# One more odd product on VectorE in the scan steps that begin from zero

## The chip, the cores and the metric

The kernel runs on one core of one Trainium2 chip. The metric is the device time of one execution in microseconds (us); lower is better. Engines are named as in the profile: PE is TensorE's matmul and PEld its weight load, DVE is VectorE, ACT is ScalarE, POOL is GpSimd, SP is SyncE, which issues the DMAs.

## The reference, cut to what matters

Two layers work on 16 images of 64 x 64 points and 96 channels, in fp32. The first is a resampled MLP; the second is a two-dimensional selective scan. The change touches the second only. With the normalized image turned into 192 channels of a sequence of L = 4096 points, four directions k (rows and columns, each forward and backward) are scanned with 16 states per channel:

```
delta = softplus(dts + dt_bias)
h0 = zeros
def step(h, inps):
    dt, ut, bt, ct = inps
    h = exp(dt[..., None] * As[None]) * h + (dt * ut)[..., None] * bt[:, :, None, :]
    y = einsum('bkdn,bkn->bkd', h, ct)
    return h, y
```

The four results are added, normalized over the channels, gated and projected back.

## The kernel before, in words

**Steps.** The scan goes image by image. An image has 8 steps, `once`: four pieces of T = 1024 points with the two forward directions (`pair` 0), then the four pieces in reverse order with the two backward directions (`pair` 1). So 16 images make 128 steps. The first step of each direction pair, `st % NT == 0` with NT = 4, begins its scans from 0.0 (line 904); the other three begin from the column that the step before left in the small tile `new` (`states`). In this document the first step of an image (forward, line 906) is its *opening step* and the fifth (backward, line 908) its *turning step*.

**Units.** A step has 6 blocks (`bi`) of 4 units (`j` = 0 to 3, four states of the 16 each). They are counted 0 to 23 here, so that unit 5 is `bi` 1, `j` 1. One unit covers two groups of 32 channels, e = 0 and e = 1, and 128 partitions hold 32 channels times 4 states. Its work is:

- `drive` (line 897, POOL): b = dtu x B, 128 x 2048, made two units ahead, in one of four buffers.
- `decay` (line 891, ACT): da = exp(delta x A), 128 x 1024 for each e, into PSUM. There is one PSUM buffer for each e, so the next unit's decay waits until this unit's da has been read for the last time.
- `recur` (lines 906 and 908, DVE): the scan h = da x h + b, 128 x 1024, once for each e. For e = 0 the states are written over da in PSUM. For e = 1 they go over b in SBUF, except in units with `odd_here`, where they go over da too.
- The product with C: for e = 0 on DVE (line 1062). For e = 1, the "odd" product, on POOL (line 1045, into one of two `odd` buffers); only where `odd_here` holds, which is `j == 3`, on DVE (line 1052).
- `keep` (line 914): the last column of h is copied to the small tile. For e = 0 ACT does it; for e = 1 DVE, but ACT where `odd_here` holds.
- `read_out` (line 931, PE): sums over the states into a PSUM tile per block.

**Order.** The order on each engine is the order in which the loop of lines 1007 to 1086 is written. Three slots in each unit hold other work: `all_work` (the step sizes of coming blocks, lines 745 to 763: m, e, w, d on ACT, half of the sum in PE, dtu on DVE) and one background generator, `front` of the next image (group norm, MLP, convolution) or `finish` of the image before. They advance by units, not by time. In opening steps `front` comes to the group norm's end in units 10 and 11: ACT makes the scale (lines 270 to 296), PE `k_ps` (line 298), and DVE adds `shift` (line 312) between the two scans of unit 11. In turning steps ACT fills the padded image (line 501) around units 4 to 7.

**What a unit's queues look like.** Where `odd_here` does not hold, ACT's decay of the next unit's e = 1 is issued right behind this unit's first scan, and POOL has odd and then the drive of two units ahead. Where it holds, POOL has only the drive; ACT's copy and the decay of e = 1 come behind DVE's line 1052, at the place of DVE's copy.

Of the kernel before, what the change touches and what calls it, by code (L numbers as in the profile page):

```python
# [63 lines left out]
NT = L // T  # L64
NQ = 4
# [12 lines left out]
def tile_two_blocks(  # L78
# [125 lines left out]
    def send(kept=0):  # L204
        while len(put_off) > kept:
            args, kwargs = put_off.pop(0)
            nc.sync.dma_start(*args, **kwargs)
# [475 lines left out]
    def scan():  # L683


        with ExitStack() as es:
# [126 lines left out]
            def fetch_dtu(ctx, bi):  # L813
                t = p2.tile([128, 2, T], F32, name="dtu")
                for e in range(2):
                    spread(t[:, e, :], "dtu", ctx, bi, e)
                return t

            def fetch_delta(ctx, bi, e):
                t = p3.tile([128, T], F32, name="delta")  # L820
                spread(t, "delta", ctx, bi, e)
                return t
# [11 lines left out]
            def fetch_y0(lc, bi):  # L834
                y0 = yp.tile([128, 2 * QT], F32, name="y0")
                nc.sync.dma_start(out=y0, in_=ypart[lc, bi])
                return y0
# [50 lines left out]
            def decay(n, e):  # L888
                k, g = group(n, e)
                da = aps.tile([128, T], F32, name="da", tag=f"da{e}")  # L890
                nc.scalar.activation(da, deltas[n // NQ, e], AF.Exp, scale=a_s[:, k, g, units[n][2]:units[n][2] + 1])  # L891
                das[n, e] = da

            def drive(n):
                b = p4.tile([128, 2, T], F32, name="b")
                bt = bc[0, blocks[units[n][1]][2], units[n][2]]
                nc.gpsimd.tensor_mul(b, dtus[n // NQ], bt.unsqueeze(1).to_broadcast([128, 2, T]))  # L897
                bs[n] = b

            def recur(n, e, out):  # L900
                st, bi, j = units[n]
                pair = steps[st][1]
                da, b = das.pop((n, e)), bs[n][:, e, :]
                before = 0.0 if st % NT == 0 else states[bi][0][:, e, j:j + 1]
                if pair == 0:
                    nc.vector.tensor_tensor_scan(out, da, b, before, ALU.mult, ALU.add)  # L906
                else:
                    nc.vector.tensor_tensor_scan(out[:, ::-1], da[:, ::-1], b[:, ::-1], before, ALU.mult, ALU.add)  # L908

            def keep(n, e, h, copy):  # L910
                st, bi, j = units[n]
                if st % NT < NT - 1:
                    end = h[:, T - 1:T] if steps[st][1] == 0 else h[:, 0:1]
                    copy(states[bi][1][:, e, j:j + 1], end)  # L914
# [21 lines left out]
            def store(n):  # L936

                st, bi, _ = units[n]
                mi, pair, lc = steps[st]
                v, s0, r = blocks[bi]  # L940
                yt = yp.tile([128, 2, QT], F32, name="yt")
                nc.scalar.copy(yt, ys.pop(n // NQ))
                yield
                if pair == 0:
                    part = dram.tile([128, 2 * QT], F32, name="part", tag=f"part{lc}_{bi}")
                    ypart[lc, bi] = part
                    nc.sync.dma_start(out=part, in_=yt.rearrange("p e t -> p (e t)"))
                else:
                    g = s0 if v < 2 else 4
                    for q in range(NQ):  # L950
                        first = T * lc + QT * q
                        nc.sync.dma_start(
                            out=image[mi]["y"][r, 32 * g:32 * g + 64, first:first + QT].rearrange(
                                "(e c) t -> c e t", e=2
                            ),
                            in_=yt[32 * q:32 * q + 32, :, :],
                        )
# [33 lines left out]
            def slot(position):  # L991
                back = ahead_gen if ahead_gen.gen is not None else behind_gen
                next(work, None)
                back.at(position)
                if back is ahead_gen and back.gen is None and position == 2:
                    behind_gen.at(position)
# [10 lines left out]
            for n, (st, bi, j) in enumerate(units):  # L1007
                mi, pair, lc = steps[st]
                v, s0, r = blocks[bi]
                m = n // NQ  # L1010
                if n % per_image == 0:
                    image[mi]["y"] = dram.tile([2, DI, L], F32, name="y_d")
                    behind_gen.drain()
                    send()
                    ahead_gen = behind_gen = Background(None)
                    if mi + 1 < B:
                        ahead_gen = Background(front(mi + 1))
                elif n % per_image == 2 and mi > 0:
                    behind_gen = Background(finish(mi - 1))
                if j == 0:  # L1020
                    new = stp.tile([128, 2, NQ], F32, name="new", tag=f"st{bi}")
                    states[bi] = (states[bi][1] if states[bi] else None, new)

                if j == 0:
                    ahead = None
                    if bi + 1 < len(blocks):
                        ahead = ctxs[st], bi + 1
                    elif n + NQ <= last:
                        ahead = ctxs[st + 1], 0
                    if ahead:  # L1030
                        dtus[m + 1] = fetch_dtu(*ahead)


                odd_here = j == NQ - 1
                h = das[n, 1] if odd_here else bs[n][:, 1, :]
                recur(n, 1, h)
                if not odd_here:
                    decay(n + 1, 1)
                slot(0)
                if storing is not None:  # L1040
                    next(storing, 0)
                    storing = None
                if not odd_here:
                    odds[n] = po.tile([128, T], F32, name="odd")
                    nc.gpsimd.tensor_mul(odds[n], h, bc[1, r, j])  # L1045
                if n + 2 <= last:
                    drive(n + 2)

                states_of_odd, h = h, das[n, 0]
                recur(n, 0, h)  # L1050
                if odd_here:
                    nc.vector.tensor_mul(bs[n][:, 1, :], states_of_odd, bc[1, r, j])  # L1052
                    keep(n, 1, states_of_odd, nc.scalar.copy)
                    if n < last:
                        decay(n + 1, 1)
                else:
                    keep(n, 1, states_of_odd, nc.vector.tensor_copy)
                if n >= 1 and j == 0:
                    storing = store(n - 1)
                    next(storing)  # L1060
                slot(1)
                nc.vector.tensor_mul(bs[n][:, 0, :], h, bc[1, r, j])  # L1062
                keep(n, 0, h, nc.scalar.copy)
                if n < last:
                    decay(n + 1, 0)
                read_out(n)
                due = list(put_off)
                slot(2)
                for one in due:
                    if put_off and put_off[0] is one:  # L1070
                        send(len(put_off) - 1)
                if j < 2 and ahead:
                    deltas[m + 1, 1 - j] = fetch_delta(*ahead, 1 - j)
                if j == 1 and n + 3 <= last and steps[units[n + 3][0]][1] == 1:
                    st2, bi2, _ = units[n + 3]
                    y0s[steps[st2][2], bi2] = fetch_y0(steps[st2][2], bi2)


                at = n % per_step
                for what in range(2):  # L1080
                    ahead_j = at - (2 * NQ - 1 + what)
                    if 0 <= ahead_j < NQ:
                        bc[what, 1, ahead_j] = fetch_bc(ctxs[st], 1, ahead_j, what)
                    ahead_j = at - (5 * NQ - 1 + what)
                    if 0 <= ahead_j < NQ and st + 1 < len(steps):
                        bc[what, 0, ahead_j] = fetch_bc(ctxs[st + 1], 0, ahead_j, what)
# [114 lines left out]
```

## Time and profile before

| | |
|---|---|
| median of three runs | 20166.42 us (20149.25 to 20170.37) |
| the profiled execution | 20161.48 us, span 20159.7 us |
| line 897 POOL b, 128 x 2048, 3072 | 4544 ns each |
| line 1045 POOL odd, 128 x 1024, 2304 | 2366 ns each |
| lines 906, 908 DVE scans from `new`, 128 x 1024 | 2336 to 2341 ns each |
| lines 906, 908 DVE scans from 0.0, 1536 | 2277 to 2278 ns each |
| line 1062 DVE product, 3072 | 1220 ns each |
| line 1052 DVE product, 768 | 1205 ns each |
| line 914 copy: DVE 1728, ACT 2880 | 148 ns, 157 ns each |
| line 891 ACT decay, 6144 | 1116 ns each |

Rows of a timeline have the start (us from the span's start), the duration (us), engine, line, operation, output<-inputs, shapes, and in brackets the engine's idle time before the instruction with what ended it. The duration of one instruction reaches some 0.1 us into the next one of the same engine, so costs are taken from start to start. A bracket names the latest releaser that the profile can see, which is sometimes one that was long done.

### The profile page before, as it was taken

The page shows a single profiled execution, that of the slowest core. Times are in us where ns is not written, and L with a number is a line of the kernel's source. Part 1 is how long each engine was busy: PE and PEld are TensorE (multiplying, and loading weights), DVE is VectorE, ACT ScalarE, POOL GpSimd, SP SyncE. Part 2 cuts the span into 40 slices and gives each one's busy share as a digit, 9 for nine tenths or more (in the row PEclk, how much of TensorE's full clock was granted, in tenths as well). Part 3 has the DMA queues.
Part 4 walks back from the last instruction along what each step waited for, and adds up shares of the span by engine and source line. Part 5 has one row for each costly group of instructions (what it writes and reads, how often), then busy time and mean ns, then how long its engine had stood idle before and what let it go on. Part 6 is the DMA issues. An engine that isn't in the chain of part 4 may idle for free. (4 is left out here: it accounts for less than half of the span.)

```text
span 20159.7 us, 275360 instructions
## 1 busy us (share of the span) xinstructions
PE 16614.9 (82%) x98732; PEld 7202.4 (36%) x98732; DVE 19096.7 (95%) x12996; ACT 13337.4 (66%) x19798; POOL 19140.5 (95%) x5384
## 2 busy tenths in 40 slices
PE   7877888888888888888888888888888888888866
PEld 4423334343343433324333343433434333243222
DVE  1999999999999999999999999999999999999997
ACT  4666766667666666766667666676666667666554
POOL 0999999999999999999999999999999999999996
PEclk8887898988889898898988889888898888989977
DMA  2665666766667666676766667666676766767654
GB/s 88 215 231 205 231 233 219 241 220 229 232 220 247 211 238 224 226 240 215 245 216 231 235 218 243 218 230 236 219 246 208 238 224 225 243 214 243 231 204 156
DMA packets 1977337, 4478.63 MB, mean 222 GB/s; under 512 B 464798, under 2 KB 564030, under 8 KB 1973918
## 3 DMA queue, kind: packets, MB, share of 16 engines
q1 hardware_dynamic: 1975966, 4461.01, 64.9%
q8 instruction: 780, 12.78, 0.3%
q14 instruction: 591, 4.84, 0.1%
HBM read 3581.91 MB, written 878.18 MB: 221 GB/s over the span
## 5 line engine op out<-in xcount | busy, mean ns | idle before, releaser
L897 POOL TENSOR_TENSOR b<-dtu,bt 128x2048 f32<-128x2048 f32 x3072 | 13918.9, 4544 | 535.4 <-DMA dtu<-dtu_d 470.3
L891 ACT ACTIVATE da<-delta,a_s 128x1024 f32<-128x1024 f32 x6144 | 6853.0, 1116 | 2289.0 <-DVE b L1062 796.6
L1045 POOL TENSOR_TENSOR odd<-b,ct 128x1024 f32<-128x1024 f32 x2304 | 5451.7, 2366 | 323.5 <-DVE b L908 184.5
L931 PE MATMUL y<-b,fold_s 128*32 128x256 f32 x30720 | 2641.4, 439 | 2513.0 <-DVE b L1062 2493.7
L1062 DVE TENSOR_TENSOR b<-da,ct 128x1024 f32<-128x1024 f32 x3072 | 3747.6, 1220 | 13.7
L908 DVE TENSOR_TENSOR_SCAN da<-da,new,b 128x1024 f32<-128x1024 f32 x1440 | 3337.7, 2336 | 101.8 <-ACT da L891 86.1
L906 DVE TENSOR_TENSOR_SCAN da<-da,new,b 128x1024 f32<-128x1024 f32 x1440 | 3339.7, 2338 | 35.5 <-ACT da L891 15.2
L914 ACT COPY new<-da 128x1 f32<-128x1 f32 x2880 | 453.0, 157 | 3361.1 <-DVE b L1062 1827.9
L931 PEld LDWEIGHTS y<-b,fold_s 128*32 128x32 f32 x30720 | 745.0, 116 | 4733.7 <-DVE b L1062 2667.6
L908 DVE TENSOR_TENSOR_SCAN b<-da,new,b 128x1024 f32<-128x1024 f32 x864 | 2021.0, 2339 | 48.1 <-ACT da L891 47.9
L906 DVE TENSOR_TENSOR_SCAN b<-da,new,b 128x1024 f32<-128x1024 f32 x864 | 2022.6, 2341 | 0.0
L931 PE MATMUL y<-odd,fold_s 128*32 128x256 f32 x18432 | 1608.1, 422 | 125.6 <-POOL odd L1045 122.1
L534 PE MATMUL c_ps<-xgp,wtap_s 96*64 96x512 f32 (+1 forms) x4608 | 1651.8, 612 | 5.5 <-ACT xgp L501 5.5
L400 PE MATMUL h_ps<-wide,w1t_s 96*128 96x500 f32 x1920 | 1119.6, 695 | 179.8 <-ACT wide L407 100.7
L427 PE MATMUL o_ps<-w2c_s,wide 128*100 128x96 f32 x9600 | 1081.1, 279 | 96.6 <-ACT wide L407 95.3
L427 PEld LDWEIGHTS o_ps<-w2c_s,wide 128*100 128x100 f32 x9600 | 1038.7, 192 | 280.4 <-ACT wide L407 157.0
L908 DVE TENSOR_TENSOR_SCAN da<-da,b 128x1024 f32<-128x1024 f32 x480 | 1084.6, 2278 | 32.6 <-ACT da L891 21.8
L906 DVE TENSOR_TENSOR_SCAN da<-da,b 128x1024 f32<-128x1024 f32 x480 | 1085.4, 2277 | 22.4 <-ACT da L891 12.1
L755 PE MATMUL s<-w,ident_s 128*128 128x512 f32 x1534 | 946.5, 703 | 193.3 <-ACT w L753 191.5
L755 PE MATMUL s<-m,half_s 128*128 128x512 f32 x1534 | 1064.7, 783 | 1.0 <-ACT m L745 1.0
L738 PE MATMUL s<-pr,dtw_s 128*128 128x512 f32 x1536 | 1052.5, 773 | 0.0
L534 PEld LDWEIGHTS c_ps<-xgp,wtap_s 96*64 96x64 f32 (+1 forms) x4608 | 593.9, 168 | 945.4 <-issue 908.8
(141 smaller groups left out, 21917.2 us busy)
## 6 DMA issues: line engine op xcount, KB each, us to landing
dtu<-dtu_d SPq DMA_DIRECT2D x1536, 512.0 KB
delta<-delta_d SPq DMA_DIRECT2D x1536, 512.0 KB
bt<-rows SPq DMA_DIRECT2D x1024, 512.0 KB
ct<-rows SPq DMA_DIRECT2D x1024, 512.0 KB
u<-xs_d SPq DMA_DIRECT2D x1536, 256.0 KB
dtu_d<-dtu SPq DMA_DIRECT2D x767, 256.0 KB
delta_d<-delta SPq DMA_DIRECT2D x767, 256.0 KB
wide<-in_x SPq DMA_DIRECT2D x768, 128.0 KB
```

Of the source, the lines that this page charges most:

```text
L400: nc.tensor.matmul(h_ps[j], lhsT=w1t_s[:, 128 * j:128 * (j + 1)], rhs=xu.rearrange("c p q -> c (p q)"), start=True, stop=True,)
L427: nc.tensor.matmul(o_ps[:, p, :], lhsT=hsq[j][:, UPS * p:UPS * (p + 1)], rhs=w2c_s[:, j, :], start=(j == 0), stop=(j == HB - 1),)
L534: nc.tensor.matmul(c_ps[p:p + n], lhsT=wtap_s[:, tap, 128 * i:128 * i + n], rhs=xgp[:, h0:h0 + 8, dx:dx + HW], start=(tap == 0), stop=(tap ...
L738: nc.tensor.matmul(s, lhsT=dtw_s[:, pair, v, :], rhs=ctx["pr"][t], start=True, stop=False, skip_group_check=True)
L755: nc.tensor.matmul(s, lhsT=by, rhs=of, start=False, stop=(of is d), skip_group_check=True)
L891: nc.scalar.activation(da, deltas[n // NQ, e], AF.Exp, scale=a_s[:, k, g, units[n][2]:units[n][2] + 1])
L897: nc.gpsimd.tensor_mul(b, dtus[n // NQ], bt.unsqueeze(1).to_broadcast([128, 2, T]))
L906: nc.vector.tensor_tensor_scan(out, da, b, before, ALU.mult, ALU.add)
L908: nc.vector.tensor_tensor_scan(out[:, ::-1], da[:, ::-1], b[:, ::-1], before, ALU.mult, ALU.add)
L931: nc.tensor.matmul(y[32 * q:32 * q + 32, e, :], lhsT=fold_s, rhs=weighed[e][:, QT * q:QT * q + QT], start=(pair == 0 and j == 0 and e == 0 ...
L1045: nc.gpsimd.tensor_mul(odds[n], h, bc[1, r, j])
L1062: nc.vector.tensor_mul(bs[n][:, 0, :], h, bc[1, r, j])
```

## The change

`odd_here` holds in one more unit of the steps that begin from zero: unit 5 (`bi` 1, `j` 1). There the states of e = 1 are written over da in PSUM, their product with C is DVE's line 1052 instead of POOL's line 1045, the copy of their last column is ACT's instead of DVE's, and the decay of unit 6's e = 1 is issued behind that product. There are 32 such units.

```
-                odd_here = j == NQ - 1
+                odd_here = j == NQ - 1 or (st % NT == 0 and bi == 1 and j == 1)
                 h = das[n, 1] if odd_here else bs[n][:, 1, :]
                 recur(n, 1, h)
                 if not odd_here:
```

## The prediction

> **What bounds the kernel now.** I read the page's first part, then the busy time by windows for one step of each kind, then the timelines of VectorE (DVE), GpSimd (POOL) and ScalarE (ACT) around unit 5, the unit that changes. Unit numbers count the 24 of a step from 0; "opening" is a step that starts the forward scan of an image, "turning" one that starts the backward scan; only these two of eight begin from zero.
>
> The page: two engines share the first place.
>
> ```profile
> PE 16614.9 (82%) x98732; PEld 7202.4 (36%) x98732; DVE 19096.7 (95%) x12996; ACT 13337.4 (66%) x19798; POOL 19140.5 (95%) x5384
> ```
>
> The windows (stretch and its length, then busy time of each engine) of the opening step of the third image, the step behind it, and that image's turning step:
>
> ```profile
> 2892.50:3042.20 149.70, 109.54 (x806) 51.21 (x806) 145.53 (x106) 105.39 (x183) 146.38 (x43) 0.79 0.65 218
> 3042.20:3192.70 150.50, 129.75 (x946) 71.18 (x942) 148.54 (x104) 105.53 (x166) 150.50 (x43) 0.84 0.63 214
> 3490.40:3643.20 152.80, 120.37 (x668) 42.74 (x668) 145.85 (x108) 115.21 (x180) 149.61 (x43) 0.89 0.68 234
> ```
>
> The reader is to see that POOL never rests in the ordinary step (150.50 of 150.50), but idles 3.3 and 3.2 us in the two that the change touches: there POOL waits too. So what counts is where POOL next waits for DVE behind unit 5.
>
> **What is removed, added and moved.** 32 steps (two in each of 16 images) have one such unit. POOL loses one odd product: the row of line 1045 has 2366 ns, and from its start to the next start is 2.32 us (2926.54 to 2928.86). DVE loses a copy of one column and gains line 1052's product; ACT gains the copy (157 ns). The scan of e=1 now writes onto da in PSUM, so the next unit's decay of e=1 is issued behind the new product instead of behind that scan. No DMA is moved. TensorE's read-out of unit 5 follows DVE's last product instead of POOL's odd: from 2928.9 to about 2929.1, in the turning step from 3531.6 to 3532.9; nothing near waits for it.
>
> DVE in units 3, 4 (start) and 5 of that opening step; unit 3 has the form that unit 5 gets:
>
> ```profile
> 2913.78 1.20 DVE L1052 TENSOR_TENSOR b<-da,ct 128x1024 f32<-128x1024 f32 x1
> 2914.90 0.68 DVE L759 TENSOR_TENSOR dtu<-s,u 128x512 f32<-128x512 f32 x1
> 2915.50 1.21 DVE L1062 TENSOR_TENSOR b<-da,ct 128x1024 f32<-128x1024 f32 x1
> 2916.63 2.28 DVE L906 TENSOR_TENSOR_SCAN b<-da,b 128x1024 f32<-128x1024 f32 x1
> ...
> 2924.47 2.27 DVE L906 TENSOR_TENSOR_SCAN da<-da,b 128x1024 f32<-128x1024 f32 x1
> 2926.65 0.15 DVE L914 COPY new<-b 128x1 f32<-128x1 f32 x1
> 2926.78 1.22 DVE L1062 TENSOR_TENSOR b<-da,ct 128x1024 f32<-128x1024 f32 x1
> 2927.92 2.28 DVE L906 TENSOR_TENSOR_SCAN b<-da,b 128x1024 f32<-128x1024 f32 x1
> ```
>
> ACT beside it: copy and decay behind unit 3's product, then unit 5's stretch:
>
> ```profile
> 2915.02 0.16 ACT L914 COPY new<-da 128x1 f32<-128x1 f32 x1 [3.55 <-DVE b L1052]
> 2915.21 1.12 ACT L891 ACTIVATE da<-delta,a_s 128x1024 f32<-128x1024 f32 x1
> ...
> 2926.01 1.10 ACT L891 ACTIVATE da<-delta,a_s 128x1024 f32<-128x1024 f32 x1
> 2927.05 0.70 ACT L749 ACTIVATE w<-e,one_s 128x512 f32<-128x512 f32 x1
> 2927.66 0.71 ACT L750 ACTIVATE d<-e,one_s 128x512 f32<-128x512 f32 x1
> 2928.27 0.14 ACT L914 COPY new<-da 128x1 f32<-128x1 f32 x1
> 2928.44 1.12 ACT L891 ACTIVATE da<-delta,a_s 128x1024 f32<-128x1024 f32 x1
> ```
>
> DVE's delay by start-to-start times:
> - The product takes 1.12 (2913.78 to 2914.90), the copy gives back 0.13 (2926.65 to 2926.78): +0.99.
> - A new wait. The product starts at 2926.65; by unit 3's rows the decay starts 1.43 later (2915.21 - 2913.78), 2928.08, and ends 1.12 on, 2929.20. A scan that waits for a decay starts 0.10 after its end (turning step, 3526.04 to 3526.14). So unit 6's first scan starts at 2929.30, not 2927.92: +1.38. In unit 3 this wait is covered by line 759's product (0.60) between; unit 5 has none, so the wait shows with 0.39.
> - Queued behind that decay on ACT are w, d, the copy and the decay of e=0: its end is 3.55 behind the first decay's start (2926.01 to 2929.56), so 2931.63. The second scan could start at 2929.30 + 2.20 = 2931.50, and starts at 2931.66: +0.16. Sum **1.54 us**.
>
> The trace shows no product 1052 without 759 behind it, so the wait is bounded: below by 0 (d = 1.0), above by the 1.5 us that ACT's longest neighbouring pair takes (line 501, d = 3.0) if ACT were not free. I take 1.54, since ACT is idle when the product ends (its queue ends at 2926.01, in the turning step at 3530.25 against 3531.65).
>
> **What of it reaches the end, opening step.** POOL gets 2.32 ahead, but its next odd products need scans that are later. At unit 8 odd starts 1.57 after its scan's end (2943.07 to 2944.64); where it waits that is 0.13. 1.54 - 1.57 + 0.13 = +0.10: POOL's gain is gone at unit 8. From unit 6 to 10 DVE waits for nothing, and at unit 11 comes the wait that ends last:
>
> ```profile
> 2963.38 0.15 DVE L312 TENSOR_TENSOR shift<-k_ps,cb_s 96x1 f32<-96x1 f32 x1 [2.78 <-PE k_ps L298]
> ```
>
> and behind it POOL:
>
> ```profile
> 2971.08 2.35 POOL L1045 TENSOR_TENSOR odd<-b,ct 128x1024 f32<-128x1024 f32 x1 [1.56 <-PE y L931]
> ```
>
> (this odd starts 0.13 after its scan; the name in the bracket is of something long done). k_ps hangs on ACT's group norm and TensorE's queue; ACT last idled for DVE at 2946.55 (0.68 <- DVE b L1062, unit 8), so that chain inherits 1.54, and DVE's 0.50 wait for b at unit 11 does not shorten it. All engines are then 1.54 late. The first two images' opening steps have a 0.60 wait for b at unit 7 (1706.40) that takes up part: 0.94. The last image's has no such chain, but its odd of unit 16 waits for DVE (0.14): 1.54.
>
> **Turning step.** Odd products of POOL, unit 4 waiting and unit 8 almost:
>
> ```profile
> 3522.44 2.34 POOL L1045 TENSOR_TENSOR odd<-b,ct 128x1024 f32<-128x1024 f32 x1 [2.01 <-DVE b L908]
> ...
> 3547.36 2.36 POOL L1045 TENSOR_TENSOR odd<-b,ct 128x1024 f32<-128x1024 f32 x1
> ```
>
> Unit 8's scan ends at 3546.95 (3544.67 + 2.28), 0.41 ahead; 1.54 - 0.41 + 0.14 = 1.27, a little less by the other images' rows: 1.26. From there POOL works without rest to the step's end. One (from 10832.8) has unit 20 at 0.22 behind a decay wait: 1.45. The last image's has 1.6 at unit 8 and two 0.6 waits for b: POOL keeps 0.5 of its gain.
>
> The ordinary steps go on at POOL's rate, and nothing there waits for a clock time, so delays add: 13 x 1.54 + 2 x 0.94 + 1.54 + 14 x 1.26 + 1.45 - 0.5 = **42 us**. The profiled execution took 20161.5 (span 20159.7): 20203.5. It lies 4.9 below the median 20166.4, so 20208 by the median, +0.21%.
>
> The Trainium skill, "Perfetto Trace Analysis", section Identifying the Most-Contended Engine, would improve the engine of highest occupancy first; that is POOL here, and by it alone the change wins 2.32 x 32. The windows above speak against it: in these steps POOL idles.
>
> **Rivals.**
> - **POOL's 2.32 reaches the end**: -74, 20092. It needs 1.54 + 2.32 - 0.13 = 3.7 us between scan and odd at units 8 and 12. For: POOL is busy 149.6 of 152.8. Against: unit 8 has 1.57 and 0.41, unit 12 0.13.
> - **Stalls swallow DVE's delay** (not slower): if k_ps is set by ACT's and TensorE's own queues, the opening steps cost 0 to 0.5 and the turning ones 0.7 to 1.26 (d = 1.0 to 1.54): +10 to +28, mid 20185. For: ACT stands 0.43 late at unit 9's copy. Against: the 0.68 of idle ACT time at unit 8. It decides below 1.26 us a step.
> - **ACT comes later than DVE** (clearly slower): the decay of unit 6 starts 2.07 later (2926.01 to 2928.08), 0.53 more than d. If ACT's later waits at units 13 and 14 (0.9 and 1.1 us of DVE idle for da) return that in full, 32 x 0.53 = 17 to 23 more: 20225 to 20231. Against: ACT idles 1.21 at 2933.68.
>
> **How the numbers follow.** Forecast (+30 to +50) 0.60; swallowed 0.20; POOL's gain 0.08; ACT later 0.12. About 0.2%, 40 us, is what a measurement of this kernel can tell from no change. The forecast lies on that line, so I split it 0.34 slower, 0.26 within: slower 0.46, same 0.46, faster 0.08. The range leaves out POOL's gain and the ends of the others: from +6 (stalls swallow most) to +69 (ACT later, and a few us of scatter: the three runs spread 21): 20172 to 20235.
>
> **What would show it.** Right: 2272 products on line 1045 and 800 on 1052; behind unit 5's product an idle of 0.4 us of DVE <- ACT da; POOL's idle before unit 12 of opening steps grown from 1.5 to 3; opening and turning steps longer by 1.5 and 1.3, the six others alike. Wrong: turning steps shorter (POOL bound to the end), or opening steps unchanged with a shorter wait for k_ps.

## The result and the profile after

| | before | after |
|---|---|---|
| median of 15 runs each, same chip | 20166.58 us (20149.12 to 20177.75) | 20203.45 us (20187.80 to 20218.34) |
| the profiled execution, span | 20161.48, 20159.7 us | 20207.56, 20205.8 us |

The ratio is 1.0020, with a 95% interval of 1.0013 to 1.0026: +36.9 us (+26 to +52). The two profiled executions differ by 46.1 us. That is 9.2 more, since the one of before lies 5.1 below its median and the one of after 4.1 above.

The first part of the page of after (busy time, share of the span, instructions):

```profile
PE 16624.6 (82%) x98732; PEld 7217.0 (36%) x98732; DVE 19134.5 (95%) x12996; ACT 13356.2 (66%) x19830; POOL 19076.4 (94%) x5352
```

POOL has 32 instructions and 64 us less to do, and yet the span is longer. DVE has gained 38 us. Where POOL's 64 us went is in the groups of instructions (operation and count, then busy time, mean ns of one, then POOL's idle time ahead of them and who ended it). The odd product before:

```profile
L1045 POOL TENSOR_TENSOR odd<-b,ct 128x1024 f32<-128x1024 f32 x2304 | 5451.7, 2366 | 323.5 <-DVE b L908 184.5 <-DMA dtu_d<-dtu 35.8 <-issue 35.7
```

The odd product and line 1052's product after:

```profile
L1045 POOL TENSOR_TENSOR odd<-b,ct 128x1024 f32<-128x1024 f32 x2272 | 5385.2, 2370 | 437.5 <-DVE b L908 242.0 <-DVE b L906 64.9 <-DMA dtu_d<-dtu 43.6
...
L1052 DVE TENSOR_TENSOR b<-da,ct 128x1024 f32<-128x1024 f32 x800 | 965.7, 1207 | 0.0
```

There are 2272 and 800 products, as predicted. POOL's idle time ahead of its odd products was 323.5 us before and is 437.5 now: +114, which is the 64 that were saved and 50 more. The name behind an arrow is the latest releaser that the profile sees, so it is the sum that counts here.

The same two steps of the third image that the prediction shows, now by the windows of after (stretch and its length, then the busy time of PE, PEld, DVE, ACT and POOL):

```profile
2896.00:3047.70 151.70, 110.97 (x806) 51.80 (x806) 146.65 (x106) 105.73 (x185) 144.13 (x42) 0.77 0.64 215
3496.10:3650.80 154.70, 120.94 (x668) 43.24 (x668) 147.26 (x108) 115.60 (x181) 147.52 (x42) 0.88 0.66 232
```

Each is about 2 us longer, and POOL idles 7.6 and 7.2 us in them where it idled 3.3 and 3.2. POOL's busy time fell by 2.25 and 2.09; its idle time rose by 4.3 and 4.0. So POOL not only lost the time that it was given, it waits for DVE's delay on top.

DVE in unit 5 of that opening step, by the timeline of after:

```profile
2930.18 1.21 DVE L1052 TENSOR_TENSOR b<-da,ct 128x1024 f32<-128x1024 f32 x1
2931.31 1.21 DVE L1062 TENSOR_TENSOR b<-da,ct 128x1024 f32<-128x1024 f32 x1
2932.84 2.29 DVE L906 TENSOR_TENSOR_SCAN b<-da,b 128x1024 f32<-128x1024 f32 x1 [0.32 <-ACT da L891]
2935.22 2.30 DVE L906 TENSOR_TENSOR_SCAN da<-da,b 128x1024 f32<-128x1024 f32 x1
2937.42 0.15 DVE L914 COPY new<-b 128x1 f32<-128x1 f32 x1
```

The product is there, then the new wait for ACT's decay (0.32 idle; the scan starts 1.53 behind line 1062's product, which takes 1.14 where nothing waits, so the wait is 0.39 from start to start), and the second scan 2.38 behind the first instead of 2.20. Counted from the step's first unit, unit 6's first scan is 1.39 later than before, and unit 7 is 1.60 later.

POOL's odd products of units 6 and 8 by the timeline of after:

```profile
2935.20 2.35 POOL L1045 TENSOR_TENSOR odd<-b,ct 128x1024 f32<-128x1024 f32 x1 [0.60 <-DVE b L906]
...
2948.28 2.34 POOL L1045 TENSOR_TENSOR odd<-b,ct 128x1024 f32<-128x1024 f32 x1 [1.76 <-DVE b L906]
```

POOL waits twice, 2.36 in all. That is its whole saving of 2.32, spent within three units. In all 32 steps unit 8's odd now starts 0.08 behind its scan's end. The next place where POOL waits is unit 12's odd; in this step the idle time ahead of it was 1.56 before and is 3.30 now:

```profile
2976.46 2.35 POOL L1045 TENSOR_TENSOR odd<-b,ct 128x1024 f32<-128x1024 f32 x1 [3.30 <-PE y L931]
```

Over the 16 opening steps the mean of this idle time went from 1.12 to 2.43. In the turning step POOL waits ahead of the odd products of units 6 and 8, where before it waited ahead of neither:

```profile
3541.23 2.35 POOL L1045 TENSOR_TENSOR odd<-b,ct 128x1024 f32<-128x1024 f32 x1 [1.78 <-DVE b L908]
...
3554.31 2.38 POOL L1045 TENSOR_TENSOR odd<-b,ct 128x1024 f32<-128x1024 f32 x1 [1.74 <-DVE b L908]
```

Mean change of a step's length, from the start of DVE's unit 0 of each step in both traces:

| step of the image | 1 opening | 2 | 3 | 4 | 5 turning | 6 | 7 | 8 |
|---|---|---|---|---|---|---|---|---|
| after - before, us | +1.28 | +0.27 | +0.06 | +0.12 | +1.33 | -0.17 | +0.28 | -0.39 |

Times 16: opening 20.4, turning 21.3, the other six together 2.8, and 1.5 at the two ends of the program. Single opening steps scatter from -1.7 to +3.3.

### The profile page after: what moved, and what is told of

The parts are those of the page before. It is cut to its first block, busy times and chain, and to the rows that moved or that the text cites. A ratio compares the mean times of both kernels' runs of the same rounds, so it can differ in the third digit from the quotient of the medians.

```text
span 20205.8 us, 275264 instructions
## 1 busy us (share of the span) xinstructions
PE 16624.6 (82%) x98732; PEld 7217.0 (36%) x98732; DVE 19134.5 (95%) x12996; ACT 13356.2 (66%) x19830; POOL 19076.4 (94%) x5352
## 4 chain that ended last, share of the span: by engine, by line
issue 28%; DVE 24%; PE 17%; POOL 13%; DMA 9%; ACT 5%; SPq 2%; DVEq 0%; POOLq 0%; ACTq 0%
POOL b L897 9%; DVE da L906 6%; DVE da L908 6%; POOL odd L1045 4%; DVE b L1062 4%; DVE b L1052 3%; PE s L755 3%; PE y L931 3%; DMA ct<-rows 3%; PE pp L718 2%; ACT da L891 2%; DVE b L906 2%; DVE b L908 2%; DVE dtu L759 1%; PE c_ps L534 1%
## 5 line engine op out<-in xcount | busy, mean ns | idle before, releaser
L1045 POOL TENSOR_TENSOR odd<-b,ct 128x1024 f32<-128x1024 f32 x2272 | 5385.2, 2370 | 437.5 <-DVE b L908 242.0
L1062 DVE TENSOR_TENSOR b<-da,ct 128x1024 f32<-128x1024 f32 x3072 | 3750.6, 1221 | 13.7
L906 DVE TENSOR_TENSOR_SCAN da<-da,new,b 128x1024 f32<-128x1024 f32 x1440 | 3340.7, 2338 | 35.2 <-ACT da L891 15.7
L908 DVE TENSOR_TENSOR_SCAN da<-da,b 128x1024 f32<-128x1024 f32 x496 | 1120.4, 2280 | 35.7 <-POOL b L897 17.0
L906 DVE TENSOR_TENSOR_SCAN da<-da,b 128x1024 f32<-128x1024 f32 x496 | 1121.1, 2278 | 14.0 <-ACT da L891 10.9
L1052 DVE TENSOR_TENSOR b<-da,ct 128x1024 f32<-128x1024 f32 x800 | 965.7, 1207 | 0.0
```

## The experiments

Three theories. **Meetings** (the prediction's): the change costs what DVE's delay is worth where POOL next waits for a scan, and where DVE waits for `k_ps`; POOL's saving is worth nearly nothing. **Load**: POOL's load counts, and something else eats the gain. **Late decay**: the dear part is not the product but ACT's decay that is issued behind it. All edits are to the kernel before unless it is said otherwise. Each ratio is against runs of the kernel before on the same chip, and the bracket behind it is its 95% interval.

### One: POOL's relief alone

```
-                if not odd_here:
+                if not odd_here and not (st % NT == 0 and bi == 1 and j == 1):
```

> The kernel before, with POOL's odd product left out in unit 5 of the 32 opening and turning steps (the states of e = 1 are summed there without being weighed by C; nothing is given to VectorE). Theory 1 (what counts is how late VectorE's scan is where POOL next needs it): POOL idles away what it saves. Opening steps 0, because its odd product of unit 12 waits for VectorE; turning steps at most 0.3 us, because odd of unit 8 starts 0.41 us behind its scan and can't start under 0.1 behind it; sum 0 to -8 us, 20158 to 20167. Theory 2 (POOL's load sets the pace): 2.32 us in each of 32 steps, -74 us, 20092.

This kernel leaves unit 5's odd product out altogether. Measured: 20151.41 against 20164.18, ratio 0.9994 (0.9985 to 1.0003): -12.8 us (-30 to +6), where the load theory has -74 and the first theory 0 to -8. POOL's odd of unit 8 and of unit 12 by its timeline in the third opening step:

```profile
2941.82 2.34 POOL L1045 TENSOR_TENSOR odd<-b,ct 128x1024 f32<-128x1024 f32 x1 [0.79 <-DVE b L906]
...
2968.97 2.35 POOL L1045 TENSOR_TENSOR odd<-b,ct 128x1024 f32<-128x1024 f32 x1 [2.25 <-DMA dtu_d<-dtu]
```

At unit 6 POOL is 2.30 ahead. At unit 8 it waits for the scan and is 1.49 ahead. At unit 12 its odd starts 0.13 after its scan, as before, and what it still had is idle time (2.25 instead of 1.56). The steps changed by -0.05 (opening) and -0.66 (turning), and the step behind the turning one by +0.56. The load theory falls.

### Two: DVE's work alone

```
-                nc.vector.tensor_mul(bs[n][:, 0, :], h, bc[1, r, j])
+                for _ in range(2 if st % NT == 0 and bi == 1 and j == 1 else 1):
+                    nc.vector.tensor_mul(bs[n][:, 0, :], h, bc[1, r, j])
```

> The kernel before, with VectorE's product of e = 0 made twice in unit 5 of the 32 steps (same place, same result): 1.12 us more on VectorE, no decay issued later, POOL's work unchanged. Theory 1: opening steps 1.12 (0.5 in the first two), turning steps 1.12 - 0.41 + 0.08 = 0.8: +28 us, 20195. Theory 2 (VectorE has the room, POOL sets the pace): within 5 us of before. Theory 3 (the cost is the late decay on ScalarE, not the product): within 10 us of before.

Measured: 20207.84 against 20164.18, ratio 1.0021 (1.0012 to 1.0030): +43.7 (+24 to +61). POOL does all its odd products here, and ACT's decays stay where they were. DVE's extra product alone costs as much as the whole change. The 28 expected lie in the interval, but the product was dearer than the 1.12 of the sum. The profile joins the two products into one line in DVE's timeline, and the pair takes 2.40 to the next start:

```profile
2938.76 2.48 DVE L1063 TENSOR_TENSOR b<-da,ct 128x1024 f32<-128x1024 f32 x2
2941.16 2.28 DVE L906 TENSOR_TENSOR_SCAN b<-da,b 128x1024 f32<-128x1024 f32 x1
```

The second one writes the same place as the first and starts 1.26 after it, not 1.12, in all 32 steps. Opening steps changed by +1.21, turning by +1.10, and the step behind the turning one by +0.46.

### Three: the change with its decay early

To the kernel after; the lines of unit 5 stand between the two scans, and what is left is skipped at the old place:

```
+                early = odd_here and j == 1
+                if early:
+                    nc.vector.tensor_mul(bs[n][:, 1, :], states_of_odd, bc[1, r, j])
+                    keep(n, 1, states_of_odd, nc.scalar.copy)
+                    decay(n + 1, 1)
```

> The change with VectorE's new product set between the two scans of unit 5, so that ScalarE's decay of unit 6 is issued as early as before and the new wait of 0.4 to 0.5 us falls away. Theory 1: VectorE's delay is 0.99 instead of 1.54 to 1.60: opening 0.99 (0.4 in the first two), turning 0.99 - 0.41 + 0.08 = 0.66: +25 us, 20192, some 12 below the change. Theory 3 (late decay): nearly all of the loss gone, 20167 to 20175. Theory 2: -74.

Measured: 20199.38 against 20164.18, ratio 1.0018 (1.0009 to 1.0026): +35.2 (+18 to +52), the change's own cost within the noise. The wait for ACT's decay is gone, as DVE's timeline shows:

```profile
2918.65 2.29 DVE L906 TENSOR_TENSOR_SCAN da<-da,b 128x1024 f32<-128x1024 f32 x1
2920.97 1.22 DVE L1052 TENSOR_TENSOR b<-da,ct 128x1024 f32<-128x1024 f32 x1
2922.11 2.29 DVE L906 TENSOR_TENSOR_SCAN da<-da,b 128x1024 f32<-128x1024 f32 x1
2924.43 1.22 DVE L1069 TENSOR_TENSOR b<-da,ct 128x1024 f32<-128x1024 f32 x1
2925.58 2.28 DVE L906 TENSOR_TENSOR_SCAN b<-da,b 128x1024 f32<-128x1024 f32 x1
```

But a product that reads what the scan just ahead of it wrote starts 2.32 after the start of that scan (2918.65 to 2920.97). One with another instruction between follows at 2.19. This happens twice here, so the delay is 1.28 (1.60 in the change) and not the 0.99 expected. The late-decay theory had nearly all of the loss gone, +1 to +9, and falls. These runs can't exclude that the decay costs some 10 us (0.32 in each of 32 steps).

### Four: another unit

To the kernel after: the product is given in unit 21 instead of unit 5 (`bi == 5 and j == 1`).

> The change moved from unit 5 to unit 21 of the same 32 steps (bi 5 instead of bi 1). Theory 1: POOL next needs VectorE in unit 0 of the following step, where odd starts 1.5 to 1.65 us behind its scan: 1.6 - 1.6 + 0.1 is about 0, and POOL keeps at most 0.1; VectorE takes its lateness back from its waits for b: within 8 us of before, 20160 to 20175. Theory 3 (product and late decay are paid wherever they stand): +37 as in unit 5. Theory 2: -74, 20092.

Measured: 20194.79 against 20164.18, ratio 1.0013 (1.0005 to 1.0022): +30.6 (+10 to +44). That is a miss for the first theory, which had it within 8 of before, and by the total it agrees with the rival that had +37. The kinds of step tell more. In turning steps it went as the first theory had it: +0.97, and the step behind -0.80. In opening steps it was +3.23 and behind -1.40. DVE's timeline in unit 23 of an opening step names a wait that no theory had:

```profile
3047.76 0.69 DVE L759 TENSOR_TENSOR dtu<-s,u 128x512 f32<-128x512 f32 x1 [1.57 <-PE s L755]
```

DVE waits there in 15 of the 16 opening steps, 1.62 on the mean, and in two of them before (0.66 and 0.52). TensorE makes this `s` with matmuls that run at half speed. The profile has two records for each matmul of line 755. PE's timeline, before and then here (duration of two records each):

```profile
3034.14 1.12 PE L755 MATMUL s<-m,half_s 128*128 128x512 f32 x2
3035.10 1.02 PE L755 MATMUL s<-w,ident_s 128*128 128x512 f32 x2
```

```profile
3041.62 2.08 PE L755 MATMUL s<-m,half_s 128*128 128x512 f32 x2
3043.49 1.92 PE L755 MATMUL s<-w,ident_s 128*128 128x512 f32 x2
```

The granted clock is the last number but two of a window's row. The stretch of these matmuls before, then the one here (PE alone):

```profile
3035.00:3042.00 7.00, 7.00 (x55) 4.29 (x55) 7.00 (x6) 3.95 (x7) 7.00 (x3) 1.00 0.33 128
```

```profile
3036.30:3046.40 10.10, 8.65 (x18) 0.50 0.48 193
```

From start to start that is 0.43 us a record at a granted clock of 1.00, and about 0.85 here at 0.50. Ahead of them TensorE had idled 2.56 and 2.19 us for work that comes later in this order, with 1.07 of work between. So DVE's delay of 1.6 became 3.2 us of an opening step, of which the step behind gave back 1.4.

The Trainium skill, "TensorE: Matmul & The Clock Gate", Part 1, describes a gate that passes half of the clock pulses after an idle window of about 3.4 us. The factor of two between 0.43 and 0.85 agrees. The idle time does not: here the clock fell 0.7 us into the second of two idle times, each shorter than that.

### Five and six: the wait for `k_ps` put later

An extra `yield` ahead of line 310 in `front`, to put the two adds that wait for `k_ps` one unit later, in the kernel before and in the kernel after.

> The kernel before, with front's two small additions on VectorE (shift and lin, lines 312 and 313) asked for one unit later, in unit 12 instead of 11, so that k_ps is there by then. Theory 1 (opening steps are bound by that wait): VectorE's 1.6 to 3.2 us of waiting in unit 11 go, and with them POOL's idle time before units 12 and 16 (1.5 and 0.2 to 0.7): -1.5 to -2.2 us in 13 to 15 opening steps, 20135 to 20147. Rival: the wait comes back one unit later (the decay that unit 13 waits 0.9 us for, or TensorE's work behind it): within 8 us of before.

> The change together with shift and lin one unit later. Theory 1: the opening steps lose what bound VectorE's 1.6 us of delay to the end; there only the 0.1 of unit 8 is left, and the turning steps pay 1.33 on: +22 us above e6_shift_later. Rival (VectorE's delay is paid wherever it stands): +37 to +45 above e6_shift_later. Theory 2 (POOL's load sets the pace once the wait is gone): -74 against it.

Measured: 20206.37 (ratio 1.0027, 1.0015 to 1.0038) and 20209.32 (1.0032, 1.0020 to 1.0043) against 20153.46. The edit did not do what it was made for: it puts all that follows in the generator one unit later. The eighth step of an image, where by the code the rest is drained in one piece, grew by 11.4 us, and the turning and the seventh steps shrank by 2.58 and 3.98. These two kernels also compute something else than the kernel before, at a place that stays open, so their totals are not used. The opening steps of the first did get shorter by 1.05, and the steps behind them by 1.29. Between the two kernels the change costs 0.51 in opening steps and nothing (-0.07) in turning ones. As a test of the wait this is inconclusive; the cleaner edit is experiment nine.

### Seven and eight: the drive ahead of the odd product

In steps that begin from zero, POOL gets the drive of two units ahead before its odd product, so that odd comes one drive, 4.5 us, later behind its scan:

```
+                if st % NT == 0 and n + 2 <= last:
+                    drive(n + 2)
                 if not odd_here:
...
-                if n + 2 <= last:
+                if st % NT and n + 2 <= last:
```

> The kernel before, with POOL's drive of two units ahead issued ahead of the odd product in every unit of the steps that begin from zero, so that POOL has 4.5 us of work where it waited for VectorE's scan. Theory 1 (POOL's idle 3.0 us an opening and 3.2 us a turning step comes from those meetings): -1.5 to -3 us a step, 20070 to 20118. Rival: TensorE's read-out waits up to 4.5 us longer for odd, and with it all TensorE work behind, the waits of ScalarE and VectorE for it grow: 20166 or more.

> The change together with drive issued ahead of odd in the steps that begin from zero. Theory 1: POOL no longer waits for VectorE at units 6 and 8, so its 2.3 us can count until VectorE itself is the limit: -25 to +10 us against e7_drive_first, against +37 for the change in the old order. Rival (VectorE's 1.6 us is what is paid, whatever POOL's order): +30 to +45 against e7_drive_first.

Measured: 20162.24 (ratio 1.0006, 0.9997 to 1.0014) in the kernel before, and 20158.63 (1.0002, 0.9992 to 1.0011) with the change, against 20153.46. The expected gain of 50 to 95 did not come; the rival, no gain, had it right. Opening steps grew by 2.84, the steps behind them shrank by 1.34. By the mean POOL idles 2.4 and 0.0 us in opening and turning steps (3.1 and 3.3 before), but 3.3 and 2.0 in the steps behind them (1.0 and 0.2 before). A new wait stood in for the old one. Ahead of the matmuls of `s`, and so of `k_ps`, TensorE reads out unit 9, and that read-out now waits for POOL's later odd: 3.3 us on the mean of 15 opening steps, where it was 0.5. With the change it waits in the first two images alone, 0.16 and 1.46. DVE's `shift`, without the change and then with it:

```profile
2970.84 0.15 DVE L312 TENSOR_TENSOR shift<-k_ps,cb_s 96x1 f32<-96x1 f32 x1 [4.53 <-PE k_ps L298]
```

```profile
2969.54 0.15 DVE L312 TENSOR_TENSOR shift<-k_ps,cb_s 96x1 f32<-96x1 f32 x1 [2.32 <-PE k_ps L298]
```

In this order POOL's lead does reach the wait that ends last: counted from the step's first scan, `shift` comes 0.61 earlier with the change in this step, and 0.75 on the mean. And the change's cost is not seen in the total: -3.6 between the two, where the rival had +30 to +45. Each ratio is uncertain by some 18 us, so one pair is weak; the last pair below repeats it.

That total is a sum of unlike parts. With the change opening steps are 1.03 shorter, but turning steps 1.77 longer, and the steps behind those 0.88 shorter. In the turning steps POOL still meets DVE: in the third image it waits 1.09 and 0.37 for the scans of units 6 and 8, where without the change it waits for none.

### Nine and ten: the adds in a later slot of unit 11

`yield VEC` ahead of `shift` becomes `yield FILL`. That puts the two adds behind the second scan of unit 11 and moves nothing else. In the kernel before, then in the kernel after.

> The kernel before, with shift and lin still in unit 11 but behind its second scan and line 1052's product (3.3 us later on VectorE) instead of between the scans; the generator keeps its phase. Theory 1 (opening steps are bound by VectorE's wait for k_ps): the wait of 1.6 to 3.2 us is hidden; POOL's idle time before unit 12 goes: -1.0 to -2.0 us in 15 opening steps, 20135 to 20150. Rival: ScalarE's copies behind the delayed TensorE work make decay of unit 13 late by as much: within 8 us of before.

> The change together with shift and lin behind unit 11's second scan. Theory 1: the opening steps' cost falls from 1.3 to about 0.1 to 0.5 (POOL is already 0.1 late at unit 8, VectorE takes its 1.6 back from waits), the turning steps go on paying 1.33: +20 to +28 us above e10_shift_in_slot1. Rival (VectorE's 1.6 is paid wherever it stands): +40 to +50 above it. Theory 2 (POOL's load sets the pace once the wait is gone): -37 below it.

Measured: 20160.27 (ratio 0.9994, 0.9986 to 1.0003) and 20170.01 (1.0000, 0.9991 to 1.0009) against 20166.78. DVE's `shift` waits for nothing in either; the line of the first:

```profile
2958.76 0.14 DVE L312 TENSOR_TENSOR shift<-k_ps,cb_s 96x1 f32<-96x1 f32 x1
```

The first is less of a gain than expected: opening steps -1.00, but the sixth steps +0.90. By its total, -6.5, it is in the rival's range. The pair tells what was asked. With this wait gone, the change costs 0.30 in opening steps instead of 1.28, and in turning steps 1.18 where it cost 1.33: +9.7 by the medians, +28 by the two profiled executions, where +20 to +28 had been expected and +40 to +50 by the rival. The wait passes DVE's delay on in the opening steps; the total is too uncertain to say more.

### Eleven and twelve: both

The later slot and the drive first, in the kernel before and in the kernel after.

> The kernel before with both: shift and lin behind unit 11's second scan, and POOL's drive ahead of odd in the steps that begin from zero. In e7_drive_first the opening steps were 2.8 longer, because TensorE's read-out of unit 10 waited for odd and k_ps stood behind it (VectorE's wait 4.7 instead of 2.4). Theory 1: 3.3 us of that wait are hidden: 1.5 to 2.5 us a step less in the 16 opening steps than in e7_drive_first, turning steps as there: 20120 to 20145. Rival: within 8 us of e7_drive_first.

> The change with both of e12_slot1_drive_first. Theory 1: with the meetings of POOL and VectorE and the wait for k_ps loosened, the change costs nothing or gains a little: -20 to +10 us against e12_slot1_drive_first. Rival: +35 to +50 against it.

Measured: 20156.17 (ratio 0.9995, 0.9986 to 1.0004) and 20153.10 (0.9991, 0.9982 to 1.0000) against 20166.78. The second, which holds the change, is the fastest kernel of this study: 13.7 us below the kernel before, with an interval that reaches no change. Again the change costs nothing in total (-3), and again by parts: opening steps -1.41, turning steps +1.79, the steps behind those -1.24. The first fell short of the 20120 to 20145 expected: its POOL idles only 1.8 and 0.0 us in opening and turning steps by the mean, but 3.0 and 2.1 in the steps behind. The idle time was moved, not removed, and DVE still waits 0.57 for `k_ps`. Its expectation named unit 10's read-out; the one that waits is unit 9's.

## Why the prediction was right

The forecast was +42 us; +36.9 was measured, +46.1 between the profiled executions. The mechanism held: DVE's delay is priced where POOL next needs a scan and where DVE waits for `k_ps`. That the total came so near is in part luck, since the opening steps cost 3.0 less than their term and the turning steps 2.7 more.

- **DVE's delay, 1.54**: 1.60 measured. The product, the new wait and the late second scan came as worked out (unit 6's first scan +1.39 against 1.38, the second scan's part 0.21 against 0.16). That the product is the main part and not the wait is shown by experiments two and three.
- **POOL's gain is gone at unit 8**: its odd was +0.11 late there in the opening step (+0.10 predicted) and, counted from unit 4's odd, +1.26 in the turning step (1.26 predicted). Two small misses cancel in these: the delay was 0.06 larger, and POOL started 0.08 behind its scan and not 0.13 or 0.14. Shown by the idle times above and by experiment one.
- **Opening steps, 23.4**: 20.4. `k_ps` is the wait that ends last (experiment ten), but it does not inherit the delay exactly. The matmuls of `s` begin 3.66 or 3.67 us after unit 10's first scan in all 15 images, before and after: that part follows DVE. `shift` then comes 10.1 to 11.7 us after this scan, later the slower TensorE makes `s`: 11.66 with 0.87 us a matmul record in one image, 10.19 with 0.66 in another. The prediction had it as a fixed distance. That makes the single steps scatter; the means before and after are 10.93 and 10.77. By the means of 15 images DVE's delay at unit 10 is 1.44 and `shift` comes 1.28 later, and these steps grew by 1.19. The waits for it in those two images, by DVE's timeline of before:

```profile
5410.39 0.15 DVE L312 TENSOR_TENSOR shift<-k_ps,cb_s 96x1 f32<-96x1 f32 x1 [3.16 <-PE k_ps L298]
...
6630.43 0.15 DVE L312 TENSOR_TENSOR shift<-k_ps,cb_s 96x1 f32<-96x1 f32 x1 [1.65 <-PE k_ps L298]
```

- **First two images, 0.94**: DVE's delay in the second image fell from 1.47 to 0.99 behind the wait for b, as said. Their opening steps changed by -1.66 and +1.63; in the first image 1.2 of that came ahead of unit 5.
- **Turning steps, 18.6**: 21.3. The steps of 15 images have +1.47 on the mean, where 1.26 was said; the last image has -0.73 (-0.5 predicted). The rest is the third rival, by which ACT's later decay returns at the wait in unit 14. DVE's timeline there, in the third image before and then after:

```profile
3583.51 2.30 DVE L908 TENSOR_TENSOR_SCAN da<-da,b 128x1024 f32<-128x1024 f32 x1 [1.10 <-ACT da L891]
```

```profile
3591.67 2.30 DVE L908 TENSOR_TENSOR_SCAN da<-da,b 128x1024 f32<-128x1024 f32 x1 [1.51 <-ACT da L891]
```

In four of these 15 images, the third among them, the wait is 1.51 after the change; in the other eleven it is gone, which gave DVE 1.0 to 1.3 us back. What reaches the end there is POOL's lateness. Counted from unit 4's odd it is 1.23 to 1.41 at unit 8 in all 15. In the eleven it is still 1.29 on the mean at unit 22; in the four POOL waits once more ahead of unit 16's odd (0.40 to 0.52), and it is 1.88. So the third rival is right in four images, for 0.6 us of a step, which is 0.16 of the mean.
- **The other six steps alike**: 2.8 in all. The reason given, that they go at POOL's rate, holds for the second, third, fourth and sixth (POOL idle 0.0 to 1.0 us by the mean before); in the seventh and eighth POOL idles 9.9 and 8.3. That these passed the delay on too is seen in the table, not explained.
- **Readings to set right**: three products of line 1052, in the program's last step, do stand without line 759 behind them in the trace of before. The first has no copy ahead of its decay, and the next scan starts 1.32 behind line 1062's product, a wait of 0.18. ACT idles for DVE once more behind 2946.55, 0.84 ahead of its copy at 2957.84. And the upper 23 of the third rival's 17 to 23 is not worked out from any row.

Of the rivals, the first (POOL's 2.32 reaches the end) fails by experiment one: its 74 us were 12.8. So does the highest occupancy as a guide, which the Trainium skill, "Perfetto Trace Analysis", section Identifying the Most-Contended Engine, would have followed here. The second (stalls swallow the delay) asked for at most 0.5 in opening steps, which were 1.28; its +28 for the total lies at the interval's lower end. The third asked for +59 to +65, above the interval, and came true in four turning steps.

Open: where the sixth steps' +0.90 in experiment nine comes from, what makes experiment two's turning step spill 0.46 into the next, and which part of the eighth step grew in experiments five and six. The change in one kind of step alone was not tried; the means by step and experiment ten stand in for it. For the turning steps no experiment takes the meeting with POOL away: there the change costs 1.2 to 1.8 us a step in every pair but that of experiments five and six.

## What to carry to other kernels

An engine at 95% is not relieved by taking work off a place where it idles anyway: look for its next wait, and how far behind the other engine's result it starts there (0.41 and 1.57 us here, for a lead of 2.32 and a delay of 1.6). Price a moved instruction with its hand-over: here 1.12 of product made 1.60 of delay, because a buffer came free later and a decay behind it. And when a wait is loosened, ask which wait then ends last: the drive-first order only moved POOL's idle time to the next step.

## What was not expected of the hardware

On DVE, a product that reads what the scan just ahead wrote starts 2.32 us after the start of a 128x1024 scan from zero (experiment three, two such pairs in each of 32 steps). An instruction that does not starts 2.19 after it, 0.09 before the scan's recorded end (2.28). The trace of before already has such pairs: in the steps that keep no last column, line 1062 starts 2.37 after a scan from `new`, where other instructions start 2.24 after it. A product that writes the same place as the product before it starts 1.26 after it instead of about 1.13. The Trainium skill, "VectorE: DVE Perf Modes", section The DRAIN you can't avoid, says that chaining does not avoid the flush between two operations, and that an operation that is not held starts earlier; the records here overlap unless the second depends on the first, and then the price is 0.13.

TensorE's record of an fp32 128x512 matmul took 0.43 us at a granted clock of 1.00, or about 0.85 at 0.50 after idle times of some 2 us, and that reaches a VectorE-bound path: 1.57 us of wait in experiment four, and 1.6 us of scatter in `k_ps`.
